# Graph attention layer on one core: another order of TensorE's work in each group, a 68th batch of picked source rows, and 17 tiles fetched row by row by SyncE

## The chip, the core and the metric

The kernel runs on one core of a Trainium2 chip. The metric is the device time of one execution in microseconds (us), lower is better. Times of before are from three runs, and the profile is that of one execution.

## The reference

One graph attention step over 6250 nodes and 206250 edges with 64 features, four heads of 16, and then a residual and a layer norm. The edges come sorted by their destination.

```python
Qh = (x @ Wq.T + bq).reshape(n, H, D)
Kh = (x @ Wk.T + bk).reshape(n, H, D)
Vh = (x @ Wv.T + bv).reshape(n, H, D)
Ee = (edge_attr @ We.T + be).reshape(-1, H, D)
score = (Kh[src] * Qh[dst] * (1.0 / np.sqrt(D)) * Ee).sum(-1)
score = jnp.exp(jnp.clip(score, -5.0, 5.0))
msg = Vh[src] * score[..., None]
wV = jax.ops.segment_sum(msg, dst, num_segments=n)
...
x = _layernorm(x + wV)
```

So every edge needs k and v of its source (a row of 128 floats, 512 bytes, anywhere in the table), q of its destination, and its own edge value.

## The kernel before, in words

**Tiles and groups.** The edges stand in 1612 tiles of 128, eight tiles to a group, 202 groups (the last has four tiles). Groups come in steps of two; the last eight groups are steps of their own. A setup of some 50 us computes the tables in DRAM: `kv_tab` (k and v of each node), `q3_tab` (q in three bf16 parts; the rows of the profile call it `q_tab`) and `key_tab`. Then one loop (L983) runs over the groups g. Nothing is scheduled by a tool: each engine works its instructions off in the order of the code, and waits for the others by semaphores.

**Three ways to k and v of the sources.** The first five groups compute them from rows of x. For most other tiles GpSimd (POOL) issues one indirect DMA per tile (`gather_kv`, L276), which fetches 128 rows of `kv_tab` into one of five buffers `kvs`, each for one step; the gathers of a step are issued four steps ahead, each behind a TensorE instruction that `where` names. The last two tiles of certain pairs of groups (`PICKED`) are **picked** instead: 67 batches of four tiles. For a batch SyncE fetches the source numbers as a row to all partitions (`srcs`, L236), ScalarE and VectorE turn them into `from`, `over` and `odd` (L241 to L243), VectorE makes one-hot tiles `hot` (L681), and TensorE multiplies them with `parts`, which holds all of x in three bf16 parts: 25 units of three matmuls (two in the last), 74 matmuls of 128x512 (`picks`, L697; the picks and most other matmuls go through the helper `product`, so their rows say L725, and L760 in the changed kernel). VectorE selects (L703), TensorE multiplies with the weights (`picked_kv`, L709, `pick<-w,x`), and ScalarE copies k and v into the buffer (L720). `first_unit` hands out 8.75 units per group (35 units in four groups); the 67 batches end in group 192.

**A group.** For group g, VectorE multiplies k with q times edge value (`products`, L787), reduces (L789), ScalarE does clip and exp (L794, L796), VectorE weighs v (L808), and the result is cut into three bf16 parts (L822, L827). TensorE sums them by destination (`sums`, L845, per step, `room<-msg,of`), with one-hot rows `of` (L775). One group earlier, VectorE has multiplied edge values `eb` with queries `qq` (`terms`, L755), and TensorE has turned the product (`turn`, L761, `qe`). `edges` (L733, `room<-et`) makes edge values into PSUM tile `room`, ScalarE adds the bias (`biased`, L740, `eb`), and `queries` (L747, `qq`) picks q rows with `to` (L256, L262). All three run some groups ahead. `sums` and `edges` and the folds share `room`.

**TensorE's order in a group g** (L1037 to L1057): `picked_kv` if a batch is due, the first four units of picks, `turn(g+1)`, `queries(g+2)`, the rest of the picks, `fold_blocks`, `sums`, `edges(g+3)`. A pick is a full 128x128 tile; `qq` uses 126 rows by 64 columns of the array, `sums` 128 by 64, `edges` 64 by 64, the folds 128 by 64 and 128 by 31.

**VectorE's order in a group** (L1007 to L1036): `products(g)`, `take`, `terms(g+1)`, the first `hots`, `message(g)`, further `hots`, `add` (L873 to L881: the step's sums from `room` into `ring`), `add_blocks`, `picked`.

**SyncE's order in a group** (L992 to L1003): at even g the edge attributes of the groups g+6 and g+7 (`et`, 512 KB, L216), at some g a row `srcs`, then `qw` of group g+4 (L230, at an address from a register), and at even g `kb` of g+6 and g+7 (L250). The DMAs that SyncE issues take eight semaphores in turn, and each waits until the one eight places before it has landed. `et` waits also until TensorE has done `edges(g+2)`, and `kb` for ScalarE's L256 on the buffer before.

**The end.** After the last group come `sums`, the last adds and the layer norm of the last two blocks (L1093 to L1103), some 12 us.

Of the kernel before, what the change touches and what calls it, by code (L numbers as in the profile page):

```python
# [11 lines left out]
U8 = mybir.dt.uint8  # L12
# [45 lines left out]
def tiles_of(g):  # L58
    return min(G, T - g * G)
# [26 lines left out]
def when(k):  # L86

    return max(g for g in range(LEAD + 4 * k // 35 + 2) if first_unit(g) <= k)


LAST = max(m for m in range(1, NG) if when(UNITS * m - 1) + 8 < NG)
BEGIN = [when(UNITS * m) for m in range(LAST)]
READY = [when(UNITS * m + UNITS - 1) for m in range(LAST)]
PICKED = [(READY[m] + 4, READY[m] + 5) for m in range(LAST)]
ALL_PICKED = {g for pair in PICKED for g in pair}
assert len(ALL_PICKED) == 2 * LAST and min(ALL_PICKED) > XG
assert all(BEGIN[m + 1] > BEGIN[m] + 1 for m in range(LAST - 1))
# [8 lines left out]
def is_picked(g, j):  # L106

    return g in ALL_PICKED and j >= tiles_of(g) - 2


BLOCKS = (0, 24, 4), (24, 40, READY[0] + 4), (40, BIG + 1, READY[0] + 6)
# [20 lines left out]


@with_exitstack
def tile_gnn(ctx: ExitStack, tc: tile.TileContext, x, x_blocks, by_rows, xT, wT, bias, beT, weT, eT, src, src_rows, dst,
             dst_rows, out):
# [8 lines left out]
    kv_tab = dram.tile([NR, 2 * C], F32, name="kv_tab")  # L145
    q3_tab = dram.tile([NR, 3 * C], BF16, name="q3_tab")
    key_tab = dram.tile([NR2, 2 * G * P], U8, name="key_tab")
    kv_v = kv_tab.rearrange("(p b) c -> p b c", p=P)
# [4 lines left out]
    kvs = [consts.tile([P, 2 * G, 2 * C], F32, name=f"kv{i}") for i in range(KVB)]  # L153

    def kv_of(g):
# [124 lines left out]
    def lots(s):  # L280

        some = []
        for g in groups_of(s):
            js = [j for j in range(tiles_of(g)) if not is_picked(g, j)]
            some += [(g, js[:len(js) // 2]), (g, js[len(js) // 2:])]
        return some

# [16 lines left out]
    with tc.tile_pool(name="nodes", bufs=1) as nodes, \  # L304
# [172 lines left out]
        def rest_of_q():  # L477
            q, two = late.pop(0)
            nc.scalar.activation(q3[:, two, 1], q, AF.Copy)
            nc.vector.tensor_sub(q3[:, two, 2], q, q3[:, two, 1])  # L480

        for i in range(NB // CB):
            bs = slice(i * CB, (i + 1) * CB)
            kv_sb = chunks.tile([P, CB, 2 * C], F32, name="kv_sb")
            for b in range(0, CB, 2):
                two = slice(i * CB + b, i * CB + b + 2)
                ps = npsum.tile([P, 2, 3 * C], F32, name="ps")
                for u in range(2):
                    c0 = (i * CB + b + u) * P
                    mark.append(nc.tensor.matmul(ps[:, u, :], xT_sb[:, c0:c0 + P], w_sb, start=True,  # L490
                                                 stop=True))
                nc.scalar.activation(kv_sb[:, b:b + 2, :], ps[:, :, :2 * C], AF.Copy)
                q = ps[:, :, 2 * C:]
                nc.scalar.activation(q3[:, two, 0], q, AF.Copy)
                nc.vector.tensor_sub(q, q, q3[:, two, 0])
                late.append((q, two))
                if len(late) > 1:
                    rest_of_q()
                place = i, b
                if place == (0, 6):  # L500
                    numbers()
                if place == (1, 0):
                    expected()
                if place == (1, 4):
                    thirds_of()
                if place == (1, 6):
                    constants()
                if place == (2, 0):
                    three_parts(be_p, be_sb, C, G)
                if place == (2, 4):  # L510
                    nc.vector.tensor_reduce(most, rows_i, axis=AX.X, op=OP.max)
                if place == (2, 8):
                    nc.vector.tensor_reduce(least, rows_i, axis=AX.X, op=OP.min)
                if place == (3, 0):
                    weights()
                if place == (3, 8):
                    wide, one = destinations()
                if place == (4, 4):
                    masks()
                pair = (i * CB + b) // 2  # L520
                for _ in range(1 + (pair >= NB // 2 - (XG - 1) * G + NB // 2)):
                    collect(*first_tiles.pop(0))
                if place == (NB // CB - 1, 4):
                    nc.sync.dma_start(kv_v[:, i * CB:i * CB + 6, :], kv_sb[:, :6])
                    nc.sync.dma_start(key_tab, key_rows.rearrange("p i e -> p (i e)"))
            if i + 1 < NB // CB:
                nc.sync.dma_start(kv_v[:, bs, :], kv_sb)
            else:
                nc.sync.dma_start(kv_v[:, i * CB + 6:, :], kv_sb[:, 6:])
            if i == 0:  # L530
                nc.sync.dma_start(rows_i, dst_rows)
            if i == 1:
                nc.sync.dma_start(src_i[:, :KEYS], src[:, :KEYS])
                nc.sync.dma_start(x_nodes[0], by_rows[:, :30 * C])
            if i == 2:
                nc.sync.dma_start(x_nodes[1], by_rows[:, 30 * C:])
                nc.sync.dma_start(dst_i[:, :KEYS], dst[:, :KEYS])
        rest_of_q()
        pw = npsum.tile([1, 1], F32, name="ps")
        nc.tensor.matmul(pw, wide, one, start=True, stop=True)  # L540
# [86 lines left out]
    with tc.If(rv == 0) as branch:  # L627

        with tc.tile_pool(name="work", bufs=2) as work, \
# [22 lines left out]
            def rooms_of(m):  # L652

                return px[m % 2].rearrange("p (j c) -> p j c", j=BATCH)
# [62 lines left out]
            def place_kv(m):  # L717
                for i, g in enumerate(PICKED[m]):
                    n = tiles_of(g)
                    nc.scalar.activation(kv_of(g)[:, n - 2:n, :], rooms_of(m)[:, 2 * i:2 * i + 2], AF.Copy)  # L720

            mark = []

# [184 lines left out]

            def fold_blocks(i):

                for u in range(2):
                    whole = slots(4 * i + u, False)
                    for lo, hi, what in whole:
                        product(folded[u * C:(u + 1) * C, lo:hi], fold, what, start=True, stop=False,
                                skip_group_check=True)
                    for lo, hi, what in slots(4 * i + u - 1, i == len(ENDS) - 1):
                        product(folded[u * C:u * C + SHIFT, lo:hi], ident[:, C:C + SHIFT], what,
                                start=hi > max(h for _, h, _ in whole), stop=True, skip_group_check=True)

            def add_blocks(i):  # L920

# [61 lines left out]
            for g in range(NG + 1):  # L983
# [7 lines left out]
                    going = alone(going[:2] if g == groups_of(step_of[g])[0] else going[2:])  # L991
                if g % LG == 0 and g + 3 * LG < NG:  # L992
                    fetch_edges(g // LG + 3)
                if g + 1 in BEGIN[1:]:
                    fetch_sources(BEGIN.index(g + 1) + 1, work)
                if g + 4 < NG:
                    fetch_queries(g + 4)
                if g % 2 == 0 and g + 6 < NG:
                    fetch_keys(g + 6, work)
                done = [s for s in range(NS) if groups_of(s)[-1] + 2 == g]  # L1000
                parted = now and step_of[g] < WHOLE
                former = before and step_of[g - 1] < WHOLE
# [4 lines left out]
                if now:  # L1007
                    products(g, *some_of(g)[0])
                if former:
                    take(g - 1, 1)  # L1010
                if g + 1 < NG:
                    terms(g + 1)
                if now:
                    weigh(g, *some_of(g)[0])
                if g + 2 < NG:
                    biased(g + 2)
                for mc in ahead[:1]:
# [255 lines left out]
```

## Time and profile of before

| | |
|---|---|
| median of 3 runs | 1701.03 us (1699.82 to 1702.28) |
| the profiled execution | 1701.22 us, of which the span of instructions is 1699.4 us |
| TensorE matmuls (PE) | 1641.8 us busy, 97% |
| VectorE (DVE) | 1525.8 us, 90% |
| GpSimd (POOL) | 1272.5 us, 75% |
| ScalarE (ACT) | 1097.8 us, 65% |
| granted TensorE clock, mean | 0.982 |

Times in rows are in us from the span's start unless they say ns. In a row of the timeline stand start, length, engine, line, operation and the tiles (out<-in), and in brackets how long the engine had been idle and what ended it. Matmuls overlap, so the distance from one start to the next tells more than the length. A float32 matmul shows as two. In a table by windows stand the window, its length, and for each engine the busy time with the count of instructions; the last numbers are the granted clock, the share of the DMA engines and GB/s. With a line chosen, the busy time is that of this line alone. SPq is SyncE's queue.

### The profile page before, as it was taken

What the parts mean: (1) busy time and instruction counts of PE and PEld (TensorE: products, weight loads), DVE (VectorE), ACT (ScalarE), POOL (GpSimd) and SP (SyncE); (2) the same over time, 40 slices, a digit from 0 to 9 for tenths busy, and PEclk for the clock granted to TensorE, in tenths of its full rate; (3) what the DMA queues carried; (4) which work ended last, traced back from release to release, by engine and by line L of the source; (5) the groups of instructions that cost most, each with busy time, mean ns of one, the idle gap of its engine ahead of it and who ended that gap; (6) DMA issues with size and microseconds to landing.
All of it is one profiled execution on the core that took longest, in us unless ns stands there. A gap on an engine that the chain in (4) does not pass through costs nothing.

```text
span 1699.4 us, 29987 instructions
## 1 busy us (share of the span) xinstructions
PE 1641.8 (97%) x10327; PEld 818.4 (48%) x10327; DVE 1525.8 (90%) x2588; ACT 1097.8 (65%) x1860; POOL 1272.5 (75%) x1354
## 2 busy tenths in 40 slices
PE   7799999999999999999999999999999999999975
PEld 6444444444444444444444444444444444444443
DVE  5699989899989899998998998989999999889986
ACT  3676666666666666666666666666666666666664
POOL 7777777777777777777777777777777777777775
PEclk9799999999999999999999999999999999999995
DMA  6744344343443434434434344443444433434341
GB/s 195 244 123 143 99 123 123 104 124 109 114 123 104 123 108 114 124 117 123 114 108 130 99 122 122 106 124 105 117 123 117 123 111 111 123 105 130 111 116 46
DMA packets 115090, 203.90 MB, mean 120 GB/s; under 512 B 55216, under 2 KB 55961, under 8 KB 114815
## 3 DMA queue, kind: packets, MB, share of 16 engines
q1 hardware_dynamic: 71484, 113.99, 22.1%
q0 software_dynamic: 43008, 86.86, 19.3%
q8 instruction: 83, 1.36, 0.3%
q10 hardware_dynamic: 436, 1.04, 0.3%
q14 instruction: 79, 0.65, 0.1%
HBM read 194.18 MB, written 7.59 MB: 119 GB/s over the span
## 4 chain that ended last, share of the span: by engine, by line
PE 80%; DVE 7%; DMA 7%; issue 2%; ACT 2%; POOL 1%; SPq 0%; DVEq 0%; ACTq 0%; POOLq 0%
PE pick L725 59%; PE room L725 11%; PE qe L761 5%; DMA kv<-kv_tab,src_i 4%; PE qq L725 3%; DMA srcs<-in_src_rows 2%; POOL kv L276 1%; DVE prod L787 1%; DVE msg L827 1%; DVE term L755 1%; PE ps L490 1%; DVE hot L681 1%; DVE score L789 1%; DVE qe L827 1%; DVE of L775 1%
## 5 line engine op out<-in xcount | busy, mean ns | idle before, releaser
L276 POOL DMA_INDIRECT kv<-kv_tab,src_i x1304 | 1233.1, 946 | 398.1 <-issue 173.8
L725 PE MATMUL pick<-hot,parts 128*128 128x512 bf16 x4958 | 1136.4, 380 | 0.0
L725 PEld LDWEIGHTS <-parts 128*128 128x128 bf16 x4958 | 459.5, 98 | 588.1 <-issue 90.3
L681 DVE TENSOR_TENSOR hot<-from,still 128x2560 bf16<-128x2560 bf16 (+4 forms) x415 | 481.7, 1164 | 2.4 <-ACT still L796 2.4
L822 ACT ACTIVATE msg<-qe 128x512 bf16<-128x512 f32 x400 | 237.8, 594 | 170.2 <-DVE qe L808 98.8
L740 ACT ACTIVATE eb<-room,be_col 128x512 f32<-128x512 f32 x202 | 136.8, 677 | 147.1 <-PE room L725 146.6
L262 ACT ACTIVATE to<-to,one_p 126x1024 bf16<-126x1024 bf16 x198 | 226.9, 1146 | 0.0
L256 ACT ACTIVATE to<-kb,minus_row 126x1024 bf16<-126x1024 uint8 x198 | 224.7, 1135 | 0.0
L794 ACT ACTIVATE score<-score,five_p 128x32 f32<-128x32 f32 x203 | 65.1, 321 | 147.8 <-DVE score L789 145.9
L761 PE MATMUL qe<-ident,term 128*128 128x128 f32 x806 | 125.7, 279 | 28.1 <-DVE term L755 26.4
L787 DVE TENSOR_TENSOR prod<-kv,qe 128x512 f32<-128x512 f32 x203 | 137.1, 676 | 12.0 <-PE qe L761 3.7
L789 DVE TENSOR_REDUCE score<-prod 128x32 f32<-128x512 f32 x203 | 138.5, 682 | 7.0
L827 DVE TENSOR_TENSOR qe<-qe,msg 128x512 f32<-128x512 f32 x200 | 138.2, 691 | 3.9 <-ACT msg L822 3.8
L808 DVE SCALAR_TENSOR_TENSOR qe<-still,kv 128x512 f32<-128x512 f32 x200 | 138.7, 693 | 0.8 <-ACT still L796 0.8
L827 DVE TENSOR_TENSOR msg<-qe,msg 128x512 bf16<-128x512 f32 x200 | 136.6, 683 | 3.1 <-ACT msg L822 2.6
L755 DVE TENSOR_TENSOR term<-eb,qq 128x512 f32<-128x512 f32 x202 | 136.6, 676 | 3.0 <-DMA kv<-kv_tab,src_i 2.6
L725 PE MATMUL room<-et,we_sb 64*64 64x256 f32 (+1 forms) x1616 | 136.2, 408 | 0.3 <-ACT eb L740 0.2
L761 PEld LDWEIGHTS qe<-ident,term 128*128 128x128 f32 x806 | 99.9, 143 | 75.8 <-DVE term L755 41.9
L243 DVE TENSOR_SCALAR odd<-srcs 128x512 int32<-128x512 int32 x66 | 30.2, 458 | 79.4 <-DMA srcs<-in_src_rows 79.3
L725 PE MATMUL room<-msg,of 128*64 128x192 bf16 (+1 forms) x1592 | 88.6, 251 | 1.6 <-DVE y L927 1.3
L725 PEld LDWEIGHTS <-of 128*64 128x64 bf16 (+1 forms) x1600 | 67.4, 110 | 39.0 <-issue 36.6
L241 ACT ACTIVATE from<-srcs,from_row 128x512 bf16<-128x512 int32 x66 | 47.3, 717 | 60.0 <-DMA srcs<-in_src_rows 60.0
(156 smaller groups left out, 1102.9 us busy)
## 6 DMA issues: line engine op xcount, KB each, us to landing
et<-in_eT SPq DMA_DIRECT2D x100, 512.0 KB
kb<-key_tab SPq DMA_DIRECT2D x101, 252.0 KB
kv<-kv_tab,src_i POOLq DMA_INDIRECT x1304
srcs<-in_src_rows SPq DMA_DIRECT2D x67, 256.0 KB
qw<-q_tab SPq DMA_DIRECT2D x202, 15.8 KB
kv_tab<-kv_sb SPq DMA_DIRECT2D x4, 640.0 KB
q_tab<-q SPq DMA_DIRECT2D x5, 480.0 KB
out<-y SPq DMA_DIRECT2D x2, 512.0 KB
```

The lines of the kernel that those rows point to most:

```text
L256: nc.scalar.activation(TO[g][:, :n, :], KB.pop(g)[:, :n * P].rearrange("p (j e) -> p j e", j=n), AF.Square, bias=minus_row3[:3 * W])
L262: nc.scalar.activation(TO[g][:, :n, :], TO[g][:, :n, :], AF.Relu, bias=one_p[:3 * W], scale=-1.0)
L276: return nc.gpsimd.indirect_dma_start(out=kv_of(g)[:, j, :], out_offset=None, in_=kv_tab[:, :], in_offset=bass.IndirectOffsetOnAxis(ap=src ...
L681: nc.vector.tensor_tensor(HOT[k][:, lo_ - lo:hi_ - lo].rearrange("p b (a c) -> p b a c", c=2), pairs(from_)[:, None].to_broadcast(shape), ...
L725: mark.append(nc.tensor.matmul(*aps, **kw))
L755: nc.vector.tensor_mul(TERM[g][:, :n], EB.pop(g)[:, :n], qq[:, :n])
L761: nc.tensor.transpose(qe[g % 2][:, k:k + half + 1:half, :], TERM[g][:, k, :], ident)
L787: nc.vector.tensor_mul(prod, kv_of(g)[:, lo:hi, :C], qe[g % 2][:, lo:hi, :])
L789: nc.vector.tensor_reduce(SCORE[g], prod.rearrange("p g (h d) -> p g h d", h=H), axis=AX.X, op=OP.add)
L808: nc.vector.scalar_tensor_tensor(to.rearrange("p g (h d) -> p g h d", h=H), WEIGHT.pop(g)[:, :, :, None].to_broadcast([P, n, H, D]), LEAST ...
L822: nc.scalar.activation(part, left, AF.Copy)
L827: nc.vector.tensor_sub(left if i == 0 else part_of(g, 2)[1], left, part)
```

## The change

1. **TensorE**: `fold_blocks`, `sums` and `edges(g+3)` move ahead of the rest of the picks, to right behind `queries(g+2)`. To fit, VectorE's `add` and `add_blocks` move ahead of `biased`, `hots` and `message`.
2. **Folds**: the matmuls of both column halves with `fold` come first, then those with the shifted identity.
3. **Source rows**: `srcs` is fetched one group earlier.
4. **68 batches**: one more batch of 74 picks, for two tiles each of the groups 199 and 200, so four gathers fewer.
5. **Singles**: tile 0 of 17 groups (13, 24, and so on to 189) is no longer gathered. In each group SyncE loads twelve addresses into registers (L747 of the changed kernel) and issues twelve DMAs of one 512-byte row each into a tile `single` (L751), 128 rows in eleven groups; two groups later ScalarE copies the tile into the `kvs` buffer (L755). Setup gets one more small DMA and one VectorE instruction that turns row numbers into byte offsets.
6. In group 200 `products` comes behind `terms`.

Order of TensorE, in the middle of the run, a group with `sums`. Before:

```order
L761 MATMUL qe_761<-ident,term 128x2x64 x4
L725 LDWEIGHTS qw
L725 MATMUL qq<-to,qw 64x512
...
L725 MATMUL pick_755<-hot,parts 128x512
L725 LDWEIGHTS of
L725 MATMUL room<-msg,of 64x192
...
L725 MATMUL room<-et,we_sb 64x256 x4
L725 LDWEIGHTS parts
L725 MATMUL pick_755<-hot,parts 128x512
```

Left out are the second half of `qq`, 15 picks and 15 more `sums`. With the change the same place reads:

```order
L796 MATMUL qe_764<-ident,term 128x2x64 x4
L760 LDWEIGHTS qw
L760 MATMUL qq<-to,qw 64x512
...
L760 LDWEIGHTS of
L760 MATMUL room<-msg,of 64x192
...
L760 MATMUL room<-et,we_sb 64x256 x4
L760 LDWEIGHTS parts
L760 MATMUL pick_758<-hot,parts 128x512
```

No picks stand between `qq` and `room` any more, and the picks behind `room` run on into those of the next group.

Order of SyncE for an even group. Before:

```order
L216 DMA et<-in_eT 128x1024
L236 DMA srcs<-in_src_rows 128x512
L230 ISA
L230 DMA qw<-q_tab 126x64
L250 DMA kb<-key_tab 126x2048
```

With the change:

```order
L229 DMA et<-in_eT 128x1024
L249 DMA srcs<-in_src_rows 128x512
L243 ISA
L243 DMA qw<-q_tab 126x64
L263 DMA kb<-key_tab 126x2048
L747 TENSOR_LOAD single_i
L751 DMA single<-kv_tab 1x512 x12
```

An odd group has only `qw`, now and then `srcs`, and now its load and twelve rows too.

Order of VectorE in a group with `add`. Before:

```order
L789 TENSOR_REDUCE score<-prod 128x32
L827 TENSOR_TENSOR msg<-qe_760,msg 128x8x64
L755 TENSOR_TENSOR term<-eb,qq 128x512
L681 TENSOR_TENSOR hot<-from,still 128x2560
L808 SCALAR_TENSOR_TENSOR qe_761<-still,kv_68 128x512
L681 TENSOR_TENSOR hot<-from,still 128x2048
L873 TENSOR_REDUCE still<-room 128x64
L878 SCALAR_TENSOR_TENSOR ring<-still,above,ring 128x64
L881 TENSOR_SCALAR ring<-still,below 128x64
```

With the change:

```order
L824 TENSOR_REDUCE score<-prod 128x32
L862 TENSOR_TENSOR msg<-qe_763,msg 128x8x64
L790 TENSOR_TENSOR term<-eb,qq 128x512
L908 TENSOR_REDUCE still<-room 128x64
L913 SCALAR_TENSOR_TENSOR ring<-still,above,ring 128x64
L916 TENSOR_SCALAR ring<-still,below 128x64
L696 TENSOR_TENSOR hot<-from,still 128x2560
L843 SCALAR_TENSOR_TENSOR qe_764<-still,kv_67 128x512
L696 TENSOR_TENSOR hot<-from,still 128x2048
```

The read of `room` stands two instructions of `hot` and one of weighing earlier.

The diff, cut to its core:

```diff
-LAST = max(m for m in range(1, NG) if when(UNITS * m - 1) + 8 < NG)
+LAST = max(m for m in range(1, NG) if when(UNITS * m - 1) + 5 < NG)
...
-PICKED = [(READY[m] + 4, READY[m] + 5) for m in range(LAST)]
+PICKED = [(r + k, r + k + 1) for r in READY for k in [min(4, NG - 2 - r - 1)]]
...
+EACH = 12
+SPAN = -(-P // EACH)
+SINGLE = list(range(SPAN + 2, NG - 3, SPAN))
...
+            def fetch_singles(g):
+
+                i, lo = g // SPAN, g % SPAN * EACH
+                if i >= len(SINGLE):
+                    return
+                if lo == 0:
+                    SINGLES[i] = work.tile([P, 2 * C], F32, name="single")
+                hi = min(lo + EACH, P)
+                _, vs = nc.values_load_multi_w_load_instructions(
+                    single_i[i:i + 1, lo:hi], engines=[mybir.EngineType.SP], min_val=0,
+                    max_val=(NR - 1) * 2 * C * 4, skip_runtime_bounds_check_because="rows of the sources")
+                for p, v in zip(range(lo, hi), vs):
+                    nc.sync.dma_start(SINGLES[i][p:p + 1, :].bitcast(U8), kv_bytes[:, bass.ds(v, 2 * C * 4)])
+
+            def place_single(g):
+                if g in SINGLE:
+                    nc.scalar.activation(kv_of(g)[:, 0, :], SINGLES.pop(SINGLE.index(g)), AF.Copy)
...
-                if g + 1 in BEGIN[1:]:
-                    fetch_sources(BEGIN.index(g + 1) + 1, work)
+                if g + 2 in BEGIN[1:]:
+                    fetch_sources(BEGIN.index(g + 2) + 1, work)
...
+                fetch_singles(g)
...
                 if now:
                     weigh(g, *some_of(g)[0])
+                for s in done:
+                    add(s)
+                if g - 1 in FOLDS:
+                    add_blocks(FOLDS[g - 1])
...
+                place_single(g + 1)
...
-                for s in done:
-                    add(s)
-                if g - 1 in FOLDS:
-                    add_blocks(FOLDS[g - 1])
...
                 if g + 2 < NG:
                     queries(g + 2)
-                for some in two[2:]:
-                    picks(some)
-                    where.append(mark[-1])
                 if g in FOLDS:
                     fold_blocks(FOLDS[g])
                 if g - 1 in ends and now:
                     sums(ends[g - 1])
                 if g + 3 < NG:
                     edges(g + 3)
+                for some in two[2:]:
+                    picks(some)
+                    where.append(mark[-1])
```

More of the change, by code (lines that the diff above doesn't have):

```diff
@@ L108, in is_picked, with is_single @@
     return g in ALL_PICKED and j >= tiles_of(g) - 2
+EACH = 12
+SPAN = -(-P // EACH)
+SINGLE = list(range(SPAN + 2, NG - 3, SPAN))
+assert SINGLE[0] >= 10
+def is_single(g, j):
+    return g in SINGLE and j == 0
 BLOCKS = (0, 24, 4), (24, 40, READY[0] + 4), (40, BIG + 1, READY[0] + 6)
@@ L134, in tile_gnn @@
 @with_exitstack
-def tile_gnn(ctx: ExitStack, tc: tile.TileContext, x, x_blocks, by_rows, xT, wT, bias, beT, weT, eT, src, src_rows, dst,
-             dst_rows, out):
+def tile_gnn(ctx: ExitStack, tc: tile.TileContext, x, x_blocks, by_rows, xT, wT, bias, beT, weT, eT, src, src_rows,
+             src_single, dst, dst_rows, out):
     nc = tc.nc
@@ L147, in tile_gnn @@
     key_tab = dram.tile([NR2, 2 * G * P], U8, name="key_tab")
+    kv_bytes = kv_tab.rearrange("(o n) c -> o (n c)", o=1).bitcast(U8)
     kv_v = kv_tab.rearrange("(p b) c -> p b c", p=P)
@@ L153, in tile_gnn @@
     kvs = [consts.tile([P, 2 * G, 2 * C], F32, name=f"kv{i}") for i in range(KVB)]
+    single_i = consts.tile([len(SINGLE), P], I32, name="single_i")
     def kv_of(g):
@@ L283, in lots @@
         for g in groups_of(s):
-            js = [j for j in range(tiles_of(g)) if not is_picked(g, j)]
+            js = [j for j in range(tiles_of(g)) if not is_picked(g, j) and not is_single(g, j)]
             some += [(g, js[:len(js) // 2]), (g, js[len(js) // 2:])]
@@ L519, in tile_gnn @@
                     masks()
+                    nc.vector.tensor_scalar(single_i, single_i, 2 * C * 4, None, op0=OP.mult)
                 pair = (i * CB + b) // 2
@@ L537, in tile_gnn @@
                 nc.sync.dma_start(dst_i[:, :KEYS], dst[:, :KEYS])
+                nc.sync.dma_start(single_i, src_single)
         rest_of_q()
@@ L720, in place_kv @@
                     nc.scalar.activation(kv_of(g)[:, n - 2:n, :], rooms_of(m)[:, 2 * i:2 * i + 2], AF.Copy)
+            SINGLES = {}
+            def fetch_singles(g):
[13 more added lines that the diff above has]
+                    nc.scalar.activation(kv_of(g)[:, 0, :], SINGLES.pop(SINGLE.index(g)), AF.Copy)
             mark = []
@@ L909, in fold_blocks @@
             def fold_blocks(i):
+                whole = [slots(4 * i + u, False) for u in range(2)]
                 for u in range(2):
-                    whole = slots(4 * i + u, False)
-                    for lo, hi, what in whole:
+                    for lo, hi, what in whole[u]:
                         product(folded[u * C:(u + 1) * C, lo:hi], fold, what, start=True, stop=False,
                                 skip_group_check=True)
+                for u in range(2):
                     for lo, hi, what in slots(4 * i + u - 1, i == len(ENDS) - 1):
                         product(folded[u * C:u * C + SHIFT, lo:hi], ident[:, C:C + SHIFT], what,
-                                start=hi > max(h for _, h, _ in whole), stop=True, skip_group_check=True)
+                                start=hi > max(h for _, h, _ in whole[u]), stop=True,
+                                skip_group_check=True)
             def add_blocks(i):
@@ L1006, in tile_gnn @@
                     keep(g - 1, 1)
-                if now:
+                if now and g != NG - 2:
                     products(g, *some_of(g)[0])
@@ L1012, in tile_gnn @@
                     terms(g + 1)
+                if g == NG - 2:
+                    products(g, *some_of(g)[0])
                 if now:
                     weigh(g, *some_of(g)[0])
+                for s in done:
+                    add(s)
+                if g - 1 in FOLDS:
+                    add_blocks(FOLDS[g - 1])
                 if g + 2 < NG:
@@ L1261 @@
             .reshape(LAST, BATCH * P),
+        "in_src_single": padded(src, P * T).reshape(T, P)[[g * G for g in SINGLE]],
         "in_dst": whole(padded(dst, P * T, PAD).reshape(T, P).T),
```

## The prediction, made before the result was known

> **What bounds the kernel now.** First the page, for the busy shares and the group of the gathers:
>
> ```profile
> PE 1641.8 (97%) x10327; PEld 818.4 (48%) x10327; DVE 1525.8 (90%) x2588; ACT 1097.8 (65%) x1860; POOL 1272.5 (75%) x1354
> L276 POOL DMA_INDIRECT kv<-kv_tab,src_i x1304 | 1233.1, 946 | 398.1 <-issue 173.8
> ```
>
> PE looks like the only full engine, but the second row says otherwise: 1304 gathers hold POOL for 1233.1 us and are followed by 398.1 us of idle time, together 1.251 us each. Whether that idle time is a wait or the cost of issuing is told by windows. Of the line of the gathers alone (length, busy, count):
>
> ```profile
> 1100.00:1600.00 500.00, 378.29 (x400) 1.00 0.41 117
> 1630.00:1660.00 30.00, 22.64 (x24) 0.94 0.37 104
> 1660.00:1690.00 30.00, 19.81 (x21) 0.61 0.21 55
> ```
>
> 400 in 500 us and 24 in 30 us are the same 1.25 us, in the body and in the tail. So POOL never waits; its 75% is full. Of all engines (PE, PEld, DVE, ACT, POOL), and of the line `prod`, one per group:
>
> ```profile
> 1100.00:1600.00 500.00, 497.03 (x3183) 240.62 (x3181) 462.61 (x767) 330.30 (x543) 378.29 (x400) 1.00 0.41 117
> 1660.00:1690.00 30.00, 16.24 (x98) 11.33 (x96) 22.74 (x55) 14.20 (x30) 19.81 (x21) 0.61 0.21 55
> ...
> 120.00:1600.00 1480.00, 124.16 (x183) 1.00 0.41 117
> ```
>
> In the body PE is full, 497 of 500 us, and sets 1480/183 = 8.1 us per group. A group needs 6.6 gathers on average (eight less four per 2.86 groups), 8.25 us: POOL loses some 0.15 us per group and eats up the lead of four steps. In the tail PE has half its time free. Who waits there is told by the timeline, POOL and DVE:
>
> ```profile
> 1680.09 0.94 POOL L276 DMA_INDIRECT kv<-kv_tab,src_i  x1 [0.30 <-issue]
> 1685.08 0.95 POOL L276 DMA_INDIRECT kv<-kv_tab,src_i  x1 [0.30 <-issue]
> ...
> 1683.09 0.69 DVE L787 TENSOR_TENSOR prod<-kv,qe 128x512 f32<-128x512 f32 x1 [3.13 <-issue]
> 1687.25 0.28 DVE L787 TENSOR_TENSOR prod<-kv,qe 128x128 f32<-128x128 f32 x1
> ```
>
> DVE idles 3.13 us until 2.1 us after the last gather of group 200 ended (1681.03), and group 201 begins 1.2 us after the very last gather. So two engines bound the time: PE for 190 groups, then POOL, which ends last. A change pays in full only if it relieves both.
>
> **POOL.** The change removes 4 + 17 = 21 gathers: 21 x 1.251 = 26.3 us. Nothing else shortens POOL's row, so the profiled execution's 1701.2 us can't fall below 1701.2 - 26.3 = **1674.9 us**. (It stands 0.2 us over the median; I make no difference.)
>
> **PE in the body.** The timeline of one group, PE:
>
> ```profile
> 806.40 0.63 PE L761 MATMUL qe<-ident,term 128*128 128x128 f32 x4
> 806.96 0.41 PE L725 MATMUL qq<-to,qw 126*64 126x512 bf16 x2
> 807.30 3.41 PE L725 MATMUL pick<-hot,parts 128*128 128x512 bf16 x15
> 810.64 0.85 PE L725 MATMUL room<-msg,of 128*64 128x192 bf16 x16
> 811.42 0.66 PE L725 MATMUL room<-et,we_sb 64*64 64x256 f32 x8
> ...
> 813.01 2.75 PE L725 MATMUL pick<-hot,parts 128*128 128x512 bf16 x12
> 815.60 0.60 PE L761 MATMUL qe<-ident,term 128*128 128x128 f32 x4
> ```
>
> Start to start, 12 picks and the step to `qe` take 2.59 us, 0.216 each: between full tiles a step is free. 15 picks and the step to `room` take 3.34 us, 0.10 more than 15 x 0.216: going to a 64-column tile costs 0.10. From `qq` back to picks takes 0.34, of which 0.216 is a 512-column product: 0.12. Today each group goes into the narrow tiles twice (`qq`, then `room`); the change joins them. Removed: 0.12 + 0.10; added: the step from `qq` to `room`, which the trace doesn't have. Between 0 (two narrow tiles) and 0.22 (as dear as what goes) I take 0.10, the nearest step into a narrow tile. That leaves 0.12 us for some 190 groups: **23 us**, bounds 0 and 42. The Trainium skill's page "TensorEngine Tiling (Array Packing)", section "Key Properties", says that changing the tiling mode, not just the tile, drains the array; the rows agree (0.10 and 0.12). By that rule `qq` to `sums` (both 128x64) would be free and `qq` to `edges` (64x64) not, so every second group saves 0.22: 32 us in place of 23.
>
> The moved matmuls must not find new waits. `edges` overwrite what ACT's `eb` reads, and `sums` what DVE's `add` reads:
>
> ```profile
> 805.64 0.68 DVE L755 TENSOR_TENSOR term<-eb,qq 128x512 f32<-128x512 f32 x1
> 805.75 0.67 ACT L740 ACTIVATE eb<-room,be_col 128x512 f32<-128x512 f32 x1
> ...
> L873 DVE TENSOR_REDUCE still<-room x97: 366/367/367, 101.8 to 1650.9; 128x64 f32<-128x192 f32 x97
> ```
>
> `qe` waits for `term`, which ends at 806.32; `eb` ends at 806.42; `room` would come at 807.30 at the earliest (behind `qe` and `qq`, 0.90). In a group with `add` (0.37, now straight behind `term`, with `eb` behind it) that is 806.3 + 0.4 + 0.7 = 807.4: a stall of 0.1 us at worst. I count nothing. Without this cover it would be some 0.7 us in each second group, 65 us, and the saving gone.
>
> **Source rows and folds.**
>
> ```profile
> DVE odd L243 <- DMA srcs<-in_src_rows: 79.3, 35, 3.7
> ...
> PE qe L761 <- DVE term L755: 5.7, 11, 1.0
> ...
> L725 PE MATMUL room<-ring,fold 128*64 128x128 f32 x92 | 19.9, 297 | 0.0
> L725 PE MATMUL room<-ring,ident 128*31 128x128 f32 x68 | 13.8, 284 | 0.0
> ```
>
> DVE waits 79.3 us for `srcs`; fetched a group (8 us) earlier, against a longest wait of 3.7, that goes. But in the body (window 120 to 1625) PE waits only 5.7 us for DVE, so it is worth **6 us**; the rest is DVE's margin, which is needed: 462.6 of 500 us busy at 8.1 us per group is 94.5% at 7.95. Fold order: 22 folds lose two tile changes of 0.10 each and some overlap: **4 us**, bounds 0 and 12.
>
> Body: 23 + 6 + 4 = **33 us** (bounds 5 and 60).
>
> **The 68th batch** adds 74 picks x 0.216 = 16.0 us and `pick<-w,x`, 1.0 us, to PE, and 25 units of `hot`, some 7.6 us, to DVE:
>
> ```profile
> L681 DVE TENSOR_TENSOR hot<-from,still 128x2560 bf16<-128x2560 bf16 (+4 forms) x415 | 481.7, 1164 | 2.4 <-ACT still L796 2.4
> ...
> 0.00:1629.00 1629.00, 130.43 (x192) 0.99 0.43 122
> ...
> 1630.00:1660.00 30.00, 3.54 (x6) 0.94 0.37 104
> ```
>
> (481.7 plus a little for `over`, over 1675 units, 0.3 us each.) By the windows of `prod`, group 192 starts at 1629, and from there on groups take 30/6 = 5 us; I use 5.6 for a group without picks. With the batch, 192 to 194 take 8.1 as in the body and 195 some 6.5, the rest 5.6: nine groups in 59 us. Compute alone would start group 201 at 1629 - 33 + 59 = 1655; POOL allows it at 1687.25 - 26.3 = 1661. So POOL decides by 6 us, and the time is its floor, 1675. Since 33 is uncertain by about that, I add 2: **1677 us**.
>
> **SyncE** pays for the singles: 2176 DMAs, 23.3 per two groups, and two register loads.
>
> ```profile
> 813.12 0.34 SPq L250 DMA_DIRECT2D kb<-key_tab  x1
> 813.55 0.36 SPq L236 DMA_DIRECT2D srcs<-in_src_rows  x1
> 814.09 0.33 SPq L230 DMA_DIRECT2D qw<-q_tab  x1
> 828.51 0.36 SPq L216 DMA_DIRECT2D et<-in_eT  x1
> ...
> L224 SPq TENSOR_LOAD <-base x26: 527/628/1248, 56.0 to 1611.8; - x26
> ...
> 1.39 3.57 DMA w_sb<-in_bias
> ...
> 568.30 4.73 DMA srcs<-in_src_rows
> ```
>
> From 814.4 to 828.5 SyncE idles: 14 us of 16. A plain DMA takes 0.43 us from start to start, one with its address computed (`qw`) 0.54. Singles have the address ready in a register: 23.3 x 0.43 = 10.0, loads 2 x 0.75 = 1.5 (twelve values, the row's median has eight), the old DMAs 2.4: 13.9 us per two groups, against 15.9. Each DMA also waits for the one eight places before it. The only one-row DMA that the chain shows landed after 3.57 us, and eight issues take 3.4: no wait to speak of. Behind a large one (4.73) a stall of 1 to 2 us per pair. So SyncE is nearly full but hidden; nothing waits, as `kb` and `qw` are fetched two groups early or more. The skill's page "DMA: Bandwidth & Descriptors", section "Rules for kernel authors", speaks against such DMAs: small transfers pay mostly overhead, some 2 us each. With eight in flight that is an estimated 0.25 us per row, below the 0.43 of issuing, and the sum stays; the row's 3.57 gives 0.45, hardly more.
>
> ACT's 17 copies (`kv<-pick` has 385 ns) and the setup's two instructions hide: ACT is 330 of 500 us busy.
>
> **Rivals.** (a) *TensorE's saving fails*: `qq` to `room` costs 0.22, or DVE at 95% holds PE up. Then the body gives 7 us, compute starts group 201 at 1629 - 7 + 59 = 1681, and the time is 1681 + 14 = 1695 us. For it: the step isn't in the trace. Against: a drain once instead of twice.
> (b) *SyncE becomes the bound, and the kernel slower.* If a single costs what `qw` does, 0.54, a pair takes 12.6 + 1.5 + 2.4 = 16.5 us: 0.6 us over 15.9, over 93 pairs 56 us, less the 16 us that fetches run ahead: 1677 + 40 = 1717 us, and 93 us more for each us beyond. It decides from 16.1 us per pair on, 0.52 per single. For it: 87% full by my count, before stalls. Against: the plain rows at 0.43.
>
> **How the numbers follow.** Forecast (1672 to 1686): 0.60. Rival (a), 1688 to 1700: 0.17. Rival (b), 1700 and up: 0.23. About 0.2%, 3.4 us, can be told from no change: faster 0.60 + 0.11 = 0.71, same 0.06, slower 0.23. The range starts at 1671, since POOL's floor leaves little below, and reaches through (a) and the near half of (b) to 1714.
>
> **What would show it.** Gathers at 1.25 us to the end, 1283 of them, the last one near 1659; `prod` still waiting for them in the last two groups; picks of one group running into the next without a step and groups at 7.95 us; no `odd <- srcs`; SyncE idle 1 to 3 us per pair, waiting at `et`. Wrong if POOL has gaps or `prod` never waits (PE decides), or if ACT waits for `kb` or `single`, or PE for `qw` (SyncE decides).

## The result and the profile after

The changed kernel takes **1674.54 us** (median of six runs, 1673.70 to 1676.24), before takes 1701.23 (six runs, 1699.82 to 1702.69). The ratio is 0.9844, with a 95% interval of 0.9831 to 0.9857: faster by 26.7 us. The forecast was 1677, the floor that it worked out for POOL 1674.9.

The page of the changed kernel, engines and the group of the gathers:

```profile
PE 1606.9 (96%) x10409; PEld 836.2 (50%) x10409; DVE 1526.0 (91%) x2598; ACT 1106.3 (66%) x1882; POOL 1254.1 (75%) x1333
L289 POOL DMA_INDIRECT kv<-kv_tab,src_i x1283 | 1214.4, 946 | 391.1 <-issue 191.1
```

21 gathers are gone, and the rest still cost (1214.4 + 391.1) / 1283 = 1.251 us each, as before. The busy shares of the engines have hardly moved, so they wouldn't tell that 27 us went. Windows over the line `prod` (length, busy, count, clock) do; first the kernel before, then the changed one:

```profile
160.00:840.00 680.00, 56.97 (x84) 1.00 0.41 116
840.00:1580.00 740.00, 61.82 (x91) 1.00 0.41 116
```

```profile
160.00:840.00 680.00, 59.90 (x88) 1.00 0.42 119
840.00:1580.00 740.00, 61.82 (x91) 1.00 0.42 118
```

In the first half a group now takes 680/88 = 7.7 us, where it took 8.1. In the second half the two kernels have the same speed, 8.1 us. That is the hand-over: up to about 840 us TensorE sets the pace and eats up the lead of the gathers, and from there on POOL sets it (with 44 gathers fewer, below, the second half goes on at 7.8 us per group). The waits of the changed kernel over the whole span say so too (total us, times, longest):

```profile
DVE prod L822 <- DMA kv<-kv_tab,src_i: 32.2, 15, 3.9
DVE prod L822 <- PE qe L796: 27.0, 35, 1.5
DVE prod L822 <- PE pick L760: 22.9, 12, 4.3
```

Before, `prod` waited 2.2 us for gathers (7 times). Now it is the first row. The row with `pick` seems to come from the same source, since it is gone in the run with 44 gathers fewer; the row with `qe` does not, as it is 43.7 us there. The end, in the timeline of the changed kernel, POOL's last gathers and then VectorE's last `prod`:

```profile
1658.05 0.94 POOL L289 DMA_INDIRECT kv<-kv_tab,src_i  x1 [0.30 <-issue]
1659.30 0.94 POOL L289 DMA_INDIRECT kv<-kv_tab,src_i  x1 [0.30 <-issue]
...
1656.95 0.69 DVE L822 TENSOR_TENSOR prod<-kv,qe 128x512 f32<-128x512 f32 x1 [0.31 <-DMA kv<-kv_tab,src_i]
...
1660.80 0.28 DVE L822 TENSOR_TENSOR prod<-kv,qe 128x128 f32<-128x128 f32 x1
```

The last gather ends at 1660.24 and the last group starts 0.6 us later, at 1660.80. Before, it started at 1687.25: 26.45 us earlier, and 21 x 1.251 is 26.3.

### The profile page after: what moved, and what is told of

The parts are those of the page before. It is cut to its first block, busy times and chain, and to the rows that moved or that the text cites. A ratio compares the mean times of both kernels' runs of the same rounds, so it can differ in the third digit from the quotient of the medians.

```text
span 1672.5 us, 34655 instructions
## 1 busy us (share of the span) xinstructions
PE 1606.9 (96%) x10409; PEld 836.2 (50%) x10409; DVE 1526.0 (91%) x2598; ACT 1106.3 (66%) x1882; POOL 1254.1 (75%) x1333
## 4 chain that ended last, share of the span: by engine, by line
PE 80%; DVE 8%; DMA 5%; ACT 3%; issue 2%; POOL 1%; DVEq 0%; SPq 0%; ACTq 0%; POOLq 0%
PE pick L760 60%; PE room L760 11%; PE qe L796 5%; DMA kv<-kv_tab,src_i 4%; PE qq L760 4%; DVE hot L696 2%; DVE prod L822 1%; PE ps L503 1%; DVE term L790 1%; DVE msg L862 1%; POOL kv L289 1%; DVE score L824 1%; DVE qe L843 1%; DMA et<-in_eT 0%; DVE qe L862 0%
## 5 line engine op out<-in xcount | busy, mean ns | idle before, releaser
L289 POOL DMA_INDIRECT kv<-kv_tab,src_i x1283 | 1214.4, 946 | 391.1 <-issue 191.1
L760 PEld LDWEIGHTS <-parts 128*128 128x128 bf16 x5032 | 476.8, 98 | 609.3 <-issue 77.2
L696 DVE TENSOR_TENSOR hot<-from,still 128x2560 bf16<-128x2560 bf16 (+4 forms) x421 | 487.8, 1162 | 2.5 <-ACT still L831 2.4
L760 PEld LDWEIGHTS <-of 128*64 128x64 bf16 (+1 forms) x1600 | 74.2, 110 | 15.3 <-issue 6.3
L760 PE MATMUL qq<-to,qw 126*64 126x512 bf16 x396 | 80.9, 405 | 0.0
L760 PEld LDWEIGHTS pick<-w,x 128*128 128x128 f32 x544 | 71.3, 193 | 18.2 <-ACT pick L729 8.6
```

The costliest lines, as they stand in the source:

```text
L289: return nc.gpsimd.indirect_dma_start(out=kv_of(g)[:, j, :], out_offset=None, in_=kv_tab[:, :], in_offset=bass.IndirectOffsetOnAxis(ap=src ...
L696: nc.vector.tensor_tensor(HOT[k][:, lo_ - lo:hi_ - lo].rearrange("p b (a c) -> p b a c", c=2), pairs(from_)[:, None].to_broadcast(shape), ...
L760: mark.append(nc.tensor.matmul(*aps, **kw))
```

## The experiments

Each time stands beside the kernel before on the same chip (1702.9 to 1704.5 us there, 1701.23 where the changed kernel was timed, so that a time compared with 1674.54 is uncertain by 1 to 3 us). As a measure of how far the compute has come I use the start of `prod` of the last group, 201: 1687.25 before, 1660.80 after.

### Does either half pay alone?

The first run is the kernel before with the new order of work (TensorE's and VectorE's) and the new folds only. The core of its edit:

```diff
                 if g + 2 < NG:
                     queries(g + 2)
-                for some in two[2:]:
-                    picks(some)
-                    where.append(mark[-1])
                 if g in FOLDS:
                     fold_blocks(FOLDS[g])
...
                 if g + 3 < NG:
                     edges(g + 3)
+                for some in two[2:]:
+                    picks(some)
+                    where.append(mark[-1])
...
```

> Before, with TensorE's and VectorE's new order of a group and the new order in the folds, but all 1304 gathers, 67 batches and no singles. My theory (two bounds, POOL's gathers end last): group 100's products start some 25 us earlier than the 882.9 us of before, but the gathers still run back to back at 1.25 us to the same end, so the time stays at 1699 to 1701.5 us. Rival (TensorE's row sets the time, gathers are incidental): 1665 to 1675 us.

Measured: 1704.47 us against 1704.45, ratio 1.0001 (0.9992 to 1.001). Nothing at all. In its timeline (of an execution that took 1705.41), POOL's last gather and VectorE's `prod` of groups 200 and 201:

```profile
1689.51 0.95 POOL L276 DMA_INDIRECT kv<-kv_tab,src_i  x1 [0.30 <-issue]
...
1687.40 0.69 DVE L787 TENSOR_TENSOR prod<-kv,qe 128x512 f32<-128x512 f32 x1 [4.67 <-DMA kv<-kv_tab,src_i]
1691.37 0.28 DVE L787 TENSOR_TENSOR prod<-kv,qe 128x128 f32<-128x128 f32 x1
```

Group 192 began at 1617 in place of 1629 us, but VectorE then stands 4.67 us waiting for a gather. All of TensorE's gain is given back as waiting.

The second run is the mirror image: the changed kernel with the old order and the old folds, so with 1283 gathers, 68 batches, the singles and the earlier source rows.

> The changed kernel with the old order of TensorE and VectorE in a group and of the folds; 1283 gathers, 68 batches, singles and the earlier source rows stay. My theory: POOL would allow 1674.5, but TensorE's groups take about 8.1 us again, and group 201 can't start before some 1675 to 1682 us, so the time is 1689 to 1697 us, with products waiting for TensorE and not for gathers at the end. Rival (fewer gathers pay by themselves): 1674.5 us.

Measured: 1697.12 us against 1704.45, ratio 0.995 (0.9936 to 0.9963). POOL's last gather and the last two `prod`:

```profile
1667.98 0.95 POOL L289 DMA_INDIRECT kv<-kv_tab,src_i  x1 [0.30 <-issue]
...
1680.04 0.68 DVE L822 TENSOR_TENSOR prod<-kv,qe 128x512 f32<-128x512 f32 x1
1684.07 0.28 DVE L822 TENSOR_TENSOR prod<-kv,qe 128x128 f32<-128x128 f32 x1
```

The last gather ends 15 us before group 201 starts, and no `prod` at the end waits for one: TensorE decides. So one half pays 0, the other 7 us, both together 27. The 7 us needn't come from the gathers, since TensorE decides in this run; the earlier source rows are in it too (more on this below). A sum of 7 and a whole of 27 is what two bounds close to each other look like.

### Do only the gathers count?

The third run keeps everything but the singles (their 17 tiles are gathered again, `SINGLE = []`).

> The changed kernel without singles: POOL gathers those 17 tiles as before, SyncE fetches no rows. My theory: 17 more gathers of 1.251 us at the end of POOL's row, 1674.5 + 21.3 = 1695.8 us (1694 to 1697). Rival (the singles' 2176 DMAs cost something elsewhere, so part of it is given back): 1685 to 1692 us.

Measured: 1698.98 us against 1704.45, ratio 0.9971 (0.9959 to 0.9982); times the 1701.23 of before that is 1696.3. In the traces, too, group 201 starts 21.3 us later than in the changed kernel (1682.07), and 17 x 1.251 is 21.3. The 17 gathers are worth their full price. The next takes away what SyncE does for the singles, and leaves the gathers out too:

```diff
-                if lo == 0:
-                    SINGLES[i] = work.tile([P, 2 * C], F32, name="single")
+                if not KEPT:
+                    KEPT.append(consts.tile([P, 2 * C], F32, name="single"))
+                    nc.sync.dma_start(KEPT[0], kv_tab[:P, :])
+                SINGLES[i] = KEPT[0]
+                return
...
```

> The changed kernel without the 2176 rows and the loads of their addresses: the 17 tiles take rows 0 to 127 of the table, fetched once, in place of the right k and v. Gathers stay at 1283. My theory: SyncE's work is hidden, so nothing changes, 1674.5 us (1673 to 1676.5; ratio 0.984). Rival (the rows' DMAs slow the gathers or TensorE's operands): 1665 to 1671 us, with gathers under 1.25 us apart or group 100 earlier than 847.5 us.

Measured: 1674.19 us, ratio 0.9827 (0.9811 to 0.9843), beside 1674.54 with the rows, and group 201 starts at 1660.83, as with them (1660.80). 2176 DMAs and 187 loads cost nothing that can be seen. And with 67 batches in place of 68 (`+ 8 < NG` again):

> The changed kernel with 67 batches: four tiles more are gathered, and 74 picks, 25 tiles of one-hots and the rest of a batch go. My theory: only the gathers count, 4 x 1.251 = 5.0 us more, 1679.5 us (ratio to before 0.987). Rival (the batch's 17 us of TensorE's time at the end weigh more): 1674.5 or less.

Measured: 1679.07 us, 4.5 above the changed kernel (5.0 expected); the ratio, 0.9848 (0.9827 to 0.9869), is too wide to tell that by itself, but group 201 starts at 1665.82, 5.0 us later, and on the same chip a kernel with eight gathers fewer (below) took 1670.15, 8.9 us less, where eight gathers are 10.0.

### Where would TensorE end?

To see TensorE's own end, 44 more gathers are left out, so that POOL's floor drops out of the way:

```diff
-            js = [j for j in range(tiles_of(g)) if not is_picked(g, j) and not is_single(g, j)]
+            js = [j for j in range(tiles_of(g)) if not is_picked(g, j) and not is_single(g, j)
+                  and not (20 <= g < 196 and g % 4 == 1 and j == 1)]
```

> The changed kernel without 44 of its gathers (tile 1 of every fourth group from 21 to 193): the k and v of those tiles are left out, and what the buffer held before is used in their place. With POOL's bound 55 us lower (1619.5), the time shows where TensorE and VectorE alone would end. By the prediction's own sum (33 us saved in the body) that is 1655 + 14 = 1669 us; by the changed kernel's first hundred groups (7.8 us each, carried on to the end) it is about 1640 us.

Measured: 1642.08 us against 1704.45, ratio 0.9633 (0.9618 to 0.9648). The second window over `prod`, POOL's last gather and the last `prod`:

```profile
840.00:1580.00 740.00, 64.68 (x95) 1.00 0.43 120
...
1615.18 0.95 POOL L289 DMA_INDIRECT kv<-kv_tab,src_i  x1 [0.30 <-issue]
...
1628.31 0.28 DVE L823 TENSOR_TENSOR prod<-kv,qe 128x128 f32<-128x128 f32 x1
```

The last gather is 12 us early, so 1628.31 is the end that compute sets. The forecast had it at 1655: TensorE gained 27 us more than I counted. (By the starts of `prod`, group 192 comes at 1564.9, where 1629 - 33 = 1596 was forecast, and the groups from there to 201 take 63 us and not 59.) Two more runs on top of this one, where TensorE decides and its prices show in the time, say where. With the old folds:

```diff
-                whole = [slots(4 * i + u, False) for u in range(2)]
                 for u in range(2):
-                    for lo, hi, what in whole[u]:
+                    whole = slots(4 * i + u, False)
+                    for lo, hi, what in whole:
...
-                for u in range(2):
                     for lo, hi, what in slots(4 * i + u - 1, i == len(ENDS) - 1):
...
```

> The kernel with 44 gathers left out (1642.1 us, TensorE decides), with the folds in their old order; as there, the k and v of 44 tiles are left out. By the start-to-start times of the folds in both traces, 0.71 us per fold: 22 x 0.71 = 15.6 us more, 1658 us. By the prediction's price (two steps between tiles of 0.10 in each fold): 4 us more, 1646 us.

Measured: 1657.74 us, ratio 0.9719 (0.9694 to 0.9743): 15.7 us more, group 201 at 1644.38 (16.1 more). The folds were worth four times my price. One fold in the timeline of PE, in the kernel before and in the changed one:

```profile
176.31 0.43 PE L725 MATMUL room<-ring,fold 128*64 128x128 f32 x2
176.67 0.41 PE L725 MATMUL room<-ring,ident 128*31 128x64 f32 x4
177.01 0.43 PE L725 MATMUL room<-ring,fold 128*64 128x128 f32 x2
177.37 0.40 PE L725 MATMUL room<-ring,ident 128*31 128x128 f32 x2
177.71 0.85 PE L725 MATMUL room<-msg,of 128*64 128x192 bf16 x16
```

```profile
807.72 0.41 PE L760 MATMUL qq<-to,qw 126*64 126x512 bf16 x2
807.96 0.39 PE L760 MATMUL room<-ring,fold 128*64 128x128 f32 x4
808.27 0.42 PE L760 MATMUL room<-ring,ident 128*31 128x64 f32 x6
808.62 0.85 PE L760 MATMUL room<-msg,of 128*64 128x192 bf16 x16
```

Start to start, a stretch of two `fold` takes 0.36 us and one of four 0.31; a stretch of two `ident` 0.34, one of six 0.35. A short stretch of these narrow f32 matmuls costs about 0.35 us here, with two in it or six. Four stretches (1.40 us) became two (0.66). In the run with the old folds itself, where the first `fold` comes behind `qq` as in the changed kernel, the four take 1.34 us (626.38 to 627.72): 0.68 more per fold, 15 us over 22, of the 15.7 measured.

With the source rows fetched at g+1 again:

> The kernel with 44 gathers left out (1642.1 us, TensorE decides), with the source rows fetched one group later, as before; the k and v of 44 tiles are left out. By the prediction, VectorE's waits for source rows reach TensorE for only 6 us: 1648 us. Rival (with groups of 7.8 us VectorE has no margin left, and each stall reaches the end): up to 79 us of stalls, 1670 to 1720 us.

Measured: 1641.80 us, ratio 0.9631 (0.9608 to 0.9655), beside 1642.08: nothing. VectorE's wait is still there, but small:

```profile
DVE odd L256 <- DMA srcs<-in_src_rows: 10.3, 14, 2.2
```

Before it was 79.3 us. Either edit takes nearly all of it away: with the new order and the new folds alone (the first run) 3.8 us are left, and with the old order and the earlier fetch (the second run) no such wait is left.

### Where does SyncE become the bound?

The changed kernel has SyncE idle at `et` for 3.3 us per pair of groups:

```profile
SPq L229 <- PE room L760: 294.8, 89, 15.5
```

Four runs fill that. With 16 rows per group (`EACH = 16`, 24 tiles):

> The changed kernel with 16 single rows per group in place of 12, so 24 tiles in place of 17 (every eighth group). My theory: seven gathers fewer, 7 x 1.251 = 8.8 us off POOL's row, so 1665.8 us (ratio to before 0.979), as SyncE is just not full: it works 12.4 us of a pair of groups in the changed kernel, 8 more rows of 0.323 us make 15.0, and a pair takes 15.65 to 16.2. Rival (SyncE's queue is full already, or the waits for the DMA eight places before add up): SyncE bounds the pair, each 0.1 us over it costs some 9 us, 1675 to 1700.

Measured: 1685.76 us (1682.4 to 1694.3, the highest being the profiled one) against 1702.87, ratio 0.9899 (0.9882 to 0.9917). SyncE's and ScalarE's waits in it:

```profile
SPq L229 <- PE room L760: 12.4, 11, 9.0
...
ACT to L269 <- DMA kb<-key_tab: 60.6, 40, 3.7
ACT kv L755 <- DMA single<-kv_tab: 51.1, 12, 6.1
```

SyncE hardly ever waits for TensorE any more, and ScalarE waits for what SyncE issues. Seven gathers fewer, and some 10 us slower than the changed kernel: the bound has passed to SyncE. With 15 rows (`EACH = 15`, 21 tiles):

> The changed kernel with 15 single rows per group, 21 tiles (every ninth group). My theory: four gathers fewer, 1674.5 - 5.0 = 1669.5 us (ratio to before 0.981), SyncE at 14.4 us of a pair. Rival (SyncE full): 1675 or more.

Measured: 1835.2 us against 1702.87, ratio 1.077 (1.0752 to 1.0788): 149 us slower than with 16 rows, though SyncE issues fewer. The rival's "1675 or more" covers the number, but neither theory had a reason for more time with fewer rows. The loads of the addresses, all of one line (min, median, max ns), in the changed kernel, with 16 rows and with 15:

```profile
L747 SPq TENSOR_LOAD <-single_i x187: 772/1016/1152, 74.9 to 1551.1; - x187
```

```profile
L747 SPq TENSOR_LOAD <-single_i x192: 1179/1253/1384, 75.5 to 1624.3; - x192
```

```profile
L747 SPq TENSOR_LOAD <-single_i x189: 783/3341/3608, 75.4 to 1745.0; - x189
```

12 values take 1.02 us, 16 take 1.25, 15 take 3.34. In the list of single instructions the loads that begin 0 or 60 words into the row take 1.67 us, those at 15, 30, 45, 75, 90 and 105 words 3.37, and the last one of 8 values, at 120, 0.80. If that is the cause, 15 rows must be cheap when each group's numbers begin at a multiple of 16 words:

```diff
-EACH = 12
+EACH = 15
...
-    single_i = consts.tile([len(SINGLE), P], I32, name="single_i")
+    single_i = consts.tile([len(SINGLE), 16 * SPAN], I32, name="single_i")
+    nc.vector.memset(single_i, 0)
...
-                    single_i[i:i + 1, lo:hi], engines=[mybir.EngineType.SP], min_val=0,
+                    single_i[i:i + 1, g % SPAN * 16:g % SPAN * 16 + 16], engines=[mybir.EngineType.SP], min_val=0,
```

> 15 single rows per group again (21 tiles, 1283 - 4 gathers), but each group's row numbers start at a multiple of 16 words of the table and 16 are loaded. My theory (the loss with 15 rows came from the loads, 3.37 us each in most groups where 12 values took 1.02 and 16 took 1.25, not from the rows): SyncE works 12.4 + 6 x 0.323 + 2 x 0.23 = 14.8 us of a pair, less than 15.65, POOL decides again, 1674.5 - 5.0 = 1669.5 us (ratio to before 0.981). Rival (15 rows per group are too many for SyncE or its eight DMAs in flight): 1690 or more.

Measured: **1670.15 us** against 1703.81, ratio 0.9796 (0.9775 to 0.9816), faster than both kernels. The loads take 1.25 us, SyncE waits at `et` again, and 1279 gathers decide:

```profile
L751 SPq TENSOR_LOAD <-single_i x189: 1150/1252/1412, 74.0 to 1566.3; - x189
```

```profile
SPq L230 <- PE room L764: 96.2, 42, 14.4
```

Of SyncE's idle time, a third is left. The last run loads SyncE with rows that nobody reads, nine per group:

```diff
...
+                for p, v in list(zip(range(lo, hi), vs))[:9]:
+                    nc.sync.dma_start(other[p:p + 1, :].bitcast(U8), kv_bytes[:, bass.ds(v, 2 * C * 4)])
```

> The changed kernel with 9 of the 12 single rows of each group fetched a second time into a tile that nobody reads; nothing else changes. My theory: SyncE needs 12.4 + 18 x 0.323 = 18.3 us per pair of groups, more than the 16.2 at which POOL lets the groups go, and becomes the bound of the first 187 groups: they end near 1755, the time is 1800 to 1850 us, with TensorE waiting for qw or ScalarE for kb. Rival (SyncE's issuing is hidden, or rows overlap more than the issue rows say): 1674.5 us.

Measured: 1931.55 us against 1702.87, ratio 1.1332 (1.1311 to 1.1352), 80 us above the upper end of what I expected. By the starts of `prod`, group 187 comes at 1811 and not near 1755: a pair took 18.7 us and not 18.3, which over all pairs is some 37 of these 56 us. From there to the end it took 120 us, for which I had allowed 45 to 95. Who waits is as forecast:

```profile
ACT to L269 <- DMA kb<-key_tab: 297.4, 66, 8.3
PE qq L764 <- DMA qw<-q_tab: 144.3, 72, 4.9
```

In the list of instructions, a pair of groups takes 18.7 us from one `et` to the next, and 15.6 (first half) to 16.0 (second half) in the changed kernel: 2.7 to 3.1 more. Over some 93 pairs that is 250 to 290 us, and 257 were measured against the changed kernel. This agrees with the forecast's "93 us more for each us beyond".

## Why the prediction was right, step by step

**Two bounds, POOL ends last: right, and shown.** POOL's floor of 1674.9 was met at 1674.5. The order and the folds alone pay nothing, all the rest without them 7 us. The 2 us that I added for the case that TensorE is late weren't needed. That the number came out so close is in part luck: POOL decides by 32 us (1660.80 against 1628.31) and not by the 6 forecast, and a miss of this size in TensorE's term the other way would have put TensorE last, near the time of rival (a).

**TensorE's 33 us: right sign, too small.** Group 201 by compute alone is at 1628.3 and not at 1655. Up to group 192 the body saved 64.5 us (1629.4 to 1564.9), beyond the bounds of 5 and 60. By term:

| term | forecast (bounds) | measured by the start of group 201, POOL out of the way |
|---|---|---|
| order of the group | 23 (0 to 42) | 1684.07 - 1644.38 = 39.7 |
| folds | 4 (0 to 12) | 1644.38 - 1628.31 = 16.1 |
| source rows | 6 | 0 with the new order |

The rows of the table add up to 56 (53 by the starts of group 192). The rest of the body's gain lies between the kernel before and the second run, which has the old order and the old folds: its group 192 starts at 1618.1, 11 us earlier than before. That run has the earlier source rows, but also fewer gathers and the singles; no run separates them.

For the order, the step from `qq` that I had to bound can now be read in the changed kernel (PE, a group with `edges` alone behind `qq`):

```profile
815.62 0.60 PE L796 MATMUL qe<-ident,term 128*128 128x128 f32 x4
816.15 0.41 PE L760 MATMUL qq<-to,qw 126*64 126x512 bf16 x2
816.49 0.66 PE L760 MATMUL room<-et,we_sb 64*64 64x256 f32 x8
```

From `qq` to `edges` takes 0.34 us, 0.216 of it the product: 0.12. From `qq` to `fold` (807.72 to 807.96, above) takes 0.24: 0.02, nothing. That is not my one price of 0.10 for both. By the Trainium skill's page "TensorEngine Tiling (Array Packing)", section "Key Properties", a change of the tiling mode drains the array and a change of the tile alone does not: 126x64 to 128x64 stays with tiles of 64 columns, to 64x64 the mode changes. The trace agrees, with 0.02 and 0.12. So groups with only `edges` save 0.10, the others 0.20, 28 us over 190 groups. Another 0.10 went for each of the 67 batches, 7 us, which I had missed: `picked_kv` came straight behind `edges` before and now follows picks. In the old order (the second run) and in the changed kernel:

```profile
806.26 0.66 PE L760 MATMUL room<-et,we_sb 64*64 64x256 f32 x8
806.86 1.16 PE L760 MATMUL pick<-w,x 128*128 128x128 f32 x8
807.85 2.75 PE L760 MATMUL pick<-hot,parts 128*128 128x512 bf16 x12
```

```profile
803.71 1.05 PE L760 MATMUL pick<-w,x 128*128 128x128 f32 x8
804.60 2.75 PE L760 MATMUL pick<-hot,parts 128*128 128x512 bf16 x12
```

0.99 us became 0.89. That leaves 5 us of the 39.7 that I can't assign to rows. **The folds** are the one term beyond the bounds given for it: "two tile changes of 0.10 each and some overlap" took the price from long stretches, where a short one costs 0.35 by itself. None of it, nor of the order's surplus, reached the time, since POOL decides.

**The moved `sums` and `edges` find no new wait: right.** In the window from 120 to 1600 us TensorE waits 1.1 us in all for `eb` ahead of `room`.

**The 68th batch is hidden: right**, it pays its four gathers.

**SyncE hidden: right, with prices that were off both ways.** A one-row DMA takes 0.32 us from start to start, not the 0.43 of a DMA over 128 rows, 2.5 us less per pair; a load takes 1.02, not 0.75, 0.5 us more per pair.

```profile
818.31 3.83 SPq L751 DMA_DIRECT2D single<-kv_tab  x12
825.17 0.37 SPq L229 DMA_DIRECT2D et<-in_eT  x1
```

Twelve rows in 3.83 us, and then 3.0 us of waiting at `et`. The work of a pair is 12.4 us (13.9 forecast), and the idle time, 3.3 us per pair, is a little over the 1 to 3 us that were forecast. Since the twelve rows go at full pace with eight in flight, a row lands within 8 x 0.32 = 2.6 us.

**Rival (a)** fell: the step costs 0.02 or 0.12, and not 0.22. (Its sum was off, too: without the 23 us of the order the body keeps 6 + 4 = 10 us and not 7, so 1692 us and not 1695.) **Rival (b)** is real, and lies closer than it looked: with four rows more per group SyncE decides, and with three more and loads that begin off a multiple of four words, the kernel is 132 us slower than before.

## What to carry to other kernels

When an engine that never waits ends the kernel and another is full, price both ends separately, by taking work away from each until the other decides; a change to one alone can measure as zero and still be half of a gain. An engine whose only work is to issue can take over work from a full one as long as its idle time per period covers it, and that time is to be measured in the row where it waits, not in its busy share. When the pace comes from an issuing queue, look at each kind of instruction in it, not only at the kind that was added: one address load at a bad place took as long as ten rows.

## What the hardware showed that was not expected

The time of the loads of row numbers into SyncE's registers goes with where they begin and how many there are: 8, 12 and 16 values of `single_i` that begin at a multiple of 4 words took 0.80, 1.02 and 1.25 us, 15 values at such a place 1.67, and 15 values anywhere else 3.37. A change of one number, from 16 rows to 15, cost 149 us by that, and a padded table brought it back. This is not the whole of it, since eight values of another table (`base`, L237) took 0.53 or 0.72. The Trainium skill's page "DMA: Bandwidth & Descriptors", section "Latency and other measured facts", has a floor of about 600 ns for such a load; the 0.80 us for eight values lies above it, and the 0.53 of `base` a little below. A DMA of one row of 512 bytes holds SyncE's queue for 0.23 us, one over 126 or 128 rows for 0.32 to 0.37. And a stretch of the folds' narrow f32 matmuls on TensorE costs 0.31 to 0.36 us whether it has two of them or six.
